# Where the norm steps between two layers stand in a slotted schedule, and one query block's delay for the second layer's input products

## The chip, the cores and the metric

The kernel runs on one core of one Trainium2 chip. The metric is the device time of a whole execution in microseconds, the median of several runs; less is better. All arithmetic is fp32.

## The reference

Eight batches of 2048 nodes with 256 features share one adjacency matrix of 2048 x 2048. Layer 0 is attention in which each of eight blocks of 256 keys has a softmax of its own, layer 1 a graph attention over all nodes. Each ends in a sum and a layer norm.

```python
q, k, v = x @ Wq.T + bq, x @ Wk.T + bk, x @ Wv.T + bv        # 4 heads of 64
scores = clip(q . k / 8, -10, 10); scores = -10 where not adjacent
ctx = sum over the 8 key blocks of softmax(scores in the block) @ v
out = layernorm(ctx @ Wo.T + bo + x) * gamma + beta
x1 = layernorm(x + out)                                       # layer 0 done
Wh = x1 @ W;  e = leaky_relu(s_src[i] + s_dst[j]), s from Wh and a
h = elu(softmax over adjacent j of e @ Wh)
result = layernorm(x1 + h)
```

## The kernel before, in words

**Slots.** Each batch b is worked in 64 slots (`SLOTS`). Slot s belongs to a query block q of 512 nodes (`NCH` = 4 blocks), a pair of heads and one of eight key blocks; a block q has 16 slots (`QS`), and i is the slot's number within its block. The order is written out by hand in the loop over s: no scheduler moves an instruction, and every engine takes its own in the order in which they are written.

**Work of every slot.** `scores(s + 1)` makes eight matmuls into `ps` (L377) and two clips with the mask into `pr` on VectorE (L388). `product(s, 0)` multiplies the probabilities of slot s with the values into `pc` (L412), which has one PSUM bank (`psC`), and ScalarE copies it to `raw` (L419). `exps(s + 1)` makes the exponentials on ScalarE (L400). Then `lower.step()` does a piece of layer 1 of the batch before: `make` builds three tiles `e` on VectorE (L712), 128 x 768 in the first third of a batch and 128 x 640 after, and `use` multiplies the three tiles built one slot earlier into `pa` (L732). `product(s, 1)` follows, with its copy. `normalize` divides by the softmax sums (`rd` on VectorE, L427, then two operations on GpSimd) in the next slot. So each engine has per slot: TensorE `ps`, `pc`, `pa`, `pc`; VectorE `rd`, two `pr`, three `e`; ScalarE `raw`, two exponentials, `raw`. Three times in 16 slots a unit of layer 1 closes: `dn` (VectorE, L755, L756), `hh` (ScalarE, L760), `ee` and `hp` (ScalarE, L764, L766) and `h` (VectorE, L768), in slots that follow each other.

**Steps between the layers.** While block q runs, `Between` finishes block q - 1, called group g = q - 1. Its steps are placed by tables from i to a step. `BESIDE` steps stand after the slot's `pr` on VectorE: `bias` (L512), `add` (attention output plus x, L538), `stats` of norm a (L477, L480; after its second half L485, L486 and a power on GpSimd, L487), `shift` (L516), `scale` (L544), `again` (L547), `stats` of norm b. `BEHIND` steps stand at the slot's end: `output` (eight matmuls into `po`, L527), `a.apply` and `finish` (four ScalarE operations each, L492; `finish` also stores the result to `x1D` in DRAM). `AHEAD` loads the stored block back in squares (`x1t`, eight loads of 64 KB), `turn` transposes the squares on VectorE (L283), and `values` multiplies a quarter of the group with layer 1's weights (`pw`, L571) and copies it to `waug` and `sd`. `po` and `pw` of the loop share one PSUM bank (`psM`). The context of layer 0 goes through DRAM in the same manner: `load_context` and `turn_context` (L454). Four groups make a batch; groups 0, 1 and 2 are finished in the blocks q = 1, 2 and 3, group 3 in a tail behind the 64 slots. SyncE issues all loads, in order.

**Groups of before.** All three have the same table: load in slot 12, turn in slot 14, `values` in slots 14 and 15 and in slots 0 and 1 of the next block. For group 2 the last two fall into the tail. Batch 0, which has no layer 1 beside it, has tables of its own (`BESIDE_0`, `BEHIND_0`, `AFTER_0`). In the last batch, layer 1 of the batch before stops 14 slots before the end of the loop (`LATE`).

Of the kernel before, what the change touches and what calls it, by code (L numbers as in the profile page):

```python
# [22 lines left out]
def adj_resnorm_kernel(  # L23
# [23 lines left out]
    NCH = N // CH  # L47
# [15 lines left out]
    QS = HP * NK  # L63
# [297 lines left out]
    def load_slab(s):  # L361
        q, hp, c = where[s]
        slab = slabs.tile([P, KT, CH], I8, tag="slab", name="slab")
        nc.sync.dma_start(out=slab, in_=clipD[q][:, KT * c : KT * (c + 1), :])
        slab_of[s] = slab

    def scores(s):
        q, hp, c = where[s]
        slab = slab_of.pop(s)
        cols = slice(q * CH, (q + 1) * CH)  # L370
        pss = []
        for u in range(KT):
            t = KT * c + u
            ps = two_banks([P, 2, CH], "ps")
            for k in range(2):
                rows = slice(k * D, (k + 1) * D)
                nc.tensor.matmul(  # L377
                    ps[:, k, :],
                    lhsT=kT[rows, hp, t * P : (t + 1) * P],
                    rhs=qT[rows, hp, cols],  # L380
                    start=True,
                    stop=True,
                )
            pss.append(ps)
        probs[s] = []
        for u in range(KT):
            pr = prp.tile([P, 2, CH], F32, tag="pr", name="pr")
            nc.vector.scalar_tensor_tensor(  # L388
                pr,
                pss[u],  # L390
                -CLIP,
                slab[:, u, :].unsqueeze(1).to_broadcast([P, 2, CH]),
                op0=ALU.max,
                op1=ALU.min,
            )
            probs[s].append(pr)
# [55 lines left out]
    def turn_context(q, hp):  # L452

        nc.vector.transpose(qT[:, hp, q * CH : (q + 1) * CH], sums.pop((q, hp))[:, 0, :])  # L454
# [46 lines left out]
    class Between:  # L501
# [87 lines left out]
    AHEAD = {12: lambda o: o.load()}  # L589
    BESIDE = {  # L590
        1: [lambda o: o.bias()],
        4: [lambda o: o.add((0, 1))],
        5: [lambda o: o.add((2, 3)), lambda o: o.a.stats((0, 1))],
        6: [lambda o: o.a.stats((2, 3)), lambda o: o.shift()],
        8: [lambda o: o.scale()],
        9: [lambda o: o.again(), lambda o: o.b2.stats((0, 1))],
        10: [lambda o: o.b2.stats((2, 3))],
        14: [lambda o: o.turn()],
    }
    BEHIND = {  # L600
        3: lambda o: o.output((0, 1)),
        4: lambda o: o.output((2, 3)),
        7: lambda o: o.a.apply(o.y),
        11: lambda o: o.finish(),
        14: lambda o: o.values((0,)),
        15: lambda o: o.values((1,)),
    }

    BESIDE_0 = {i: steps for i, steps in BESIDE.items() if i != 14} | {15: BESIDE[14]}
    BEHIND_0 = {i: step for i, step in BEHIND.items() if i != 14} | {15: BEHIND[14]}  # L610
    AFTER_0 = {i: lambda o, i=i: o.values((i + 1,)) for i in range(3)}
    AFTER = {0: lambda o: o.values((2,)), 1: lambda o: o.values((3,))}
# [271 lines left out]
    for b in range(B):  # L884
        waug = blocks.tile([P, NT, H, D1], F32, tag="waug", name="waug")
        sd = small.tile([P, 2 * H, NT], F32, tag="sd", name="sd", bufs=1)
        if b == 0:
            for s in range(3):
                load_slab(s)
            scores(0)  # L890
            for u in range(KT):
                exps(0, u)
        if lower:
            for _ in range(STEP):
                lower.make()
        closing = Closing(b - 2, CLOSING) if b > 1 else None
        if closing:
            closing.do(-1)
        group = None
        beside, behind, after = (BESIDE, BEHIND, AFTER) if b else (BESIDE_0, BEHIND_0, AFTER_0)  # L900
        for s in range(SLOTS):
            q, hp, c = where[s]
            i = s % QS
            send()
            if s + 3 < SLOTS:
                load_slab(s + 3)
            if i == 0:
                before = group
                group = Between(b, q - 1, sd, waug) if q else None
            if i == 1 and q:  # L910
                load_context(b, q - 1, 1)
            if i == QS // 2 + 1:
                load_context(b, q, 0)
            if group and i in AHEAD:
                AHEAD[i](group)
            if s == SLOTS - 3 and b + 1 < B:
                turns = [project(b + 1, g) for g in range(NCH)]
                turns[0].pop(0)()
            if s:
                normalize(s - 1)  # L920
            if s + 1 < SLOTS:
                scores(s + 1)

            if s == SLOTS - 1 and b + 1 < B:
                turns[0].pop(0)()
            if i == 3 and q:
                turn_context(q - 1, 1)
            if i == QS // 2 + 3:
                turn_context(q, 0)
            if group:  # L930
                for step in beside.get(i, ()):
                    step(group)
            elif closing:
                closing.do(s, behind=False)
            product(s, 0, not lower)
            if s + 1 < SLOTS:
                for u in range(KT):
                    exps(s + 1, u)
            if lower:
                if b + 1 < B or s < SLOTS - LATE:  # L940
                    lower.step()
            elif masks.left():
                masks.step()
            product(s, 1, not lower)

            if before and i in after:
                after[i](before)
            if i == 0 and q:
                send_context(b, q - 1, 1)
            if i == QS // 2:  # L950
                send_context(b, q, 0)
            if group and i in behind:
                behind[i](group)
            elif closing and not q:
                closing.do(s, beside=False)
        normalize(SLOTS - 1)

        send()
        before = group
        gd, fs = factors(b, sd, waug)  # L960
        group = None
        every = tuple(range(QT))

        def begin():
            nonlocal group
            group = Between(b, NCH - 1, sd, waug)

        def ctx():
            context(NCH - 1, 1)

        steps = [
            lambda: group.bias(),
            lambda: group.output(every),
            lambda: group.add(every),
            lambda: (group.shift(), group.a.stats(every)),
            lambda: group.a.apply(group.y),
            lambda: (group.scale(), group.again(), group.b2.stats(every)),
            lambda: group.finish(),
            lambda: group.turn_all(),
            lambda: group.values((0, 1)),  # L980
            lambda: group.values((2, 3)),
        ]
        if b + 1 < B:
            (k0, v0, q0), (l1, t1, k1, v1, q1), (l2, t2, k2, v2, q2), (l3, t3, k3, v3, q3) = turns
            rest = [lambda: lower.rest(1)] if lower else []
            first = [] if b else [lambda: before.values((1,))]
            order = [begin, *rest, l1, *rest, *first, lambda: before.values((2, 3))]
            order += [*rest, ctx, *rest, k0]
            order += [steps[0], t1, steps[1], v0, steps[2], steps[3], l2, k1, steps[4], q0]
            order += [steps[5], v1, t2, l3, steps[6], q1, steps[7], k2, steps[8], steps[9], t3, v2]  # L990
            order += [lambda: [load_slab(s) for s in range(3)], fs[0], q2, fs[1], k3, fs[2], v3]
            order += [lambda: scores(0), q3, lambda: [exps(0, u) for u in range(KT)]]
        else:

            step = lower.step
            order = [begin, lambda: before.values((2, 3)), steps[0], step, ctx, step, steps[1], step]
            order += [steps[2], step, steps[3], step, steps[4], step, steps[5], step, steps[6], step]
            order += [steps[7], step, steps[8], step, steps[9], step, fs[0], step, fs[1], step, fs[2]]
            order += [step, lambda: lower.rest(4)]
            assert sum(p is step for p in order) == LATE  # L1000
        for piece in order:
            send()
            piece()
        send()
        lower = Layer1(b, gd, waug)
# [56 lines left out]
```

## Time and profile before

| what | us |
|---|---|
| device time, median of 3 runs (3830.42 to 3833.37) | 3831.26 |
| profiled span | 3835.0 |
| TensorE busy with matmuls | 3696.8 |
| VectorE busy | 3203.6 |
| ScalarE busy | 1950.1 |
| GpSimd busy | 1385.1 |

A slot begins, in what follows, with the first `ps` matmul that is issued in it. The lengths below are the differences of those starts in the timeline of TensorE, in batch 3; the other batches with a layer 1 beside them agree within 0.03 us, up to a few single slots.

| slot i | 0 | 1 | 2 | 3 | 4 | 5 | 6 | 7 | 8 | 9 | 10 | 11 | 12 | 13 | 14 | 15 |
|---|---|---|---|---|---|---|---|---|---|---|---|---|---|---|---|---|
| q = 0 | 6.74 | 6.03 | 6.03 | 6.03 | 6.03 | 6.03 | 6.03 | 6.03 | 6.03 | 6.03 | 6.03 | 6.03 | 6.03 | 6.03 | 6.45 | 6.03 |
| q = 1 | 6.03 | 6.03 | 6.03 | 7.96 | 7.96 | 5.80 | 5.68 | 5.68 | 6.21 | 5.68 | 5.85 | 5.87 | 5.95 | 6.44 | 6.77 | 6.77 |
| q = 2 | 6.77 | 6.77 | 5.68 | 7.61 | 7.61 | 5.68 | 5.68 | 5.68 | 6.12 | 5.68 | 5.78 | 5.87 | 5.95 | 6.45 | 6.77 | 6.77 |
| q = 3 | 6.77 | 6.77 | 5.68 | 7.61 | 7.61 | 5.68 | 5.68 | 5.68 | 6.13 | 5.68 | 5.79 | 5.87 | 5.95 | 6.44 | | |

How to read the rows of the profile: busy time is the union of an engine's spans; a matmul's end is modelled, so TensorE shows as busy where it may be waiting on a weight load. In a timeline, a row gives the start, the time from the row's first start to its last end, engine, line, operation, names (output, then inputs) and count; brackets give the idle time before it and what ended it.

### The profile page before, as it was taken

Reading aid. Unit: us, or ns where it says so; the run is one execution under the profiler, and the core shown is the slowest. Engines: PE = TensorE matmul, PEld = TensorE weight load, DVE = VectorE, ACT = ScalarE, POOL = GpSimd, SP = SyncE. Lnnn points to the kernel's source line nnn. Section 1 sums busy time; section 2 is a strip of 40 time slices with the busy share of each in tenths; the row PEclk is TensorE's granted clock in tenths of the full one; section 3 lists DMA queues with packets and bytes.
Section 4 is the critical chain, followed back from the end, with each engine's and each line's share of the span. In section 5 each row is a group of like instructions: output and inputs, shape, how many; then the busy total and the mean of one; then the engine's idle time right before and its main releaser. Section 6 shows DMA issues by size and latency. Waiting matters only on the chain. (4 is left out here: it accounts for less than half of the span.)

```text
span 3835.0 us, 160246 instructions
## 1 busy us (share of the span) xinstructions
PE 3696.8 (96%) x72100; PEld 2752.3 (72%) x72100; DVE 3203.6 (84%) x4810; ACT 1950.1 (51%) x3601; POOL 1385.1 (36%) x1202
## 2 busy tenths in 40 slices
PE   9999999999999999999999999999999999999787
PEld 5656677776777777776777767777677777776676
DVE  5876499986999789995999959998699978998798
ACT  4666345555555555554555545555455555555321
POOL 1445233333433343343433324333343434334310
PEclk9999999999999999999999999999999999999999
DMA  6652333333333433333433334333333433333354
GB/s 161 151 113 65 77 101 99 96 87 112 105 95 102 91 117 101 97 101 87 131 99 92 98 92 134 97 95 88 110 110 94 104 86 118 104 99 86 93 149 123
DMA packets 756545, 398.50 MB, mean 104 GB/s; under 512 B 425744, under 2 KB 721040, under 8 KB 755856
## 3 DMA queue, kind: packets, MB, share of 16 engines
q1 hardware_dynamic: 705856, 354.54, 36.3%
q10 hardware_dynamic: 50000, 33.70, 2.7%
q8 instruction: 564, 9.24, 1.0%
q14 instruction: 125, 1.02, 0.1%
HBM read 331.22 MB, written 56.89 MB: 101 GB/s over the span
## 5 line engine op out<-in xcount | busy, mean ns | idle before, releaser
L388 DVE SCALAR_TENSOR_TENSOR pr<-ps,slab 128x1024 f32<-128x1024 f32 x1024 | 1192.5, 1205 | 215.7 <-PE ps L377 211.4
L712 DVE SCALAR_TENSOR_TENSOR e<-srow,gd,et 128x640 f32<-128x640 f32 (+1 forms) x1536 | 1349.1, 934 | 11.2 <-DMA srow<-rowD 5.7
L412 PEld LDWEIGHTS pc<-vaug,pr 128*64 128x64 f32 x32768 | 1040.6, 138 | 442.7 <-issue 253.7
L412 PE MATMUL pc<-vaug,pr 128*64 128x65 f32 x32768 | 1158.4, 224 | 40.9 <-ACT raw L419 32.0
L400 ACT ACTIVATE pr<-pr 128x1024 f32<-128x1024 f32 x1024 | 1050.4, 1057 | 158.1 <-DVE pr L388 143.6
L732 PE MATMUL pa<-waug,e 128*64 128x65 f32 x32768 | 1083.2, 224 | 41.1 <-DVE e L712 39.6
L732 PEld LDWEIGHTS pa<-waug,e 128*64 128x64 f32 x32768 | 1020.8, 139 | 67.7 <-DVE e L712 39.2
L377 PE MATMUL ps<-qT,kT 64*128 64x512 f32 x4096 | 1029.0, 619 | 3.6 <-DVE pr L388 2.6
L434 POOL TENSOR_TENSOR part<-raw,rd 128x512 f32<-128x512 f32 x448 | 467.9, 1044 | 1462.9 <-DVE rd L427 1450.4
L419 ACT COPY raw<-pc 128x260 f32<-128x260 f32 x1024 | 384.9, 377 | 1181.6 <-PE pc L412 1159.0
L377 PEld LDWEIGHTS ps<-qT,kT 64*128 64x128 f32 x4096 | 350.9, 186 | 330.7 <-issue 205.1
L436 POOL TENSOR_TENSOR acc<-acc,part 128x512 f32<-128x512 f32 x448 | 574.2, 1282 | 35.2
L427 DVE RECIPROCAL rd<-raw 128x8 f32<-128x8 f32 x512 | 100.9, 197 | 117.0 <-ACT raw L419 113.2
L434 POOL TENSOR_TENSOR acc<-raw,rd 128x512 f32<-128x512 f32 x64 | 66.8, 1043 | 336.9 <-DVE rd L427 336.1
L760 ACT ACTIVATE hh<-pa,dn 128x64 f32<-128x64 f32 x512 | 114.6, 320 | 100.6 <-DVE dn L756 96.8
L571 PE MATMUL pw<-w_sb,x1T 128*128 128x264 f32 x512 | 142.4, 415 | 8.6 <-DVE x1T L283 8.0
L487 POOL TENSOR_TENSOR rs_c<-rs_c,nhalf 128x4 f32<-128x4 f32 x32 | 55.6, 1737 | 228.4 <-DVE off_c L486 228.4
L321 PE MATMUL pp<-xT,wk_sb 128*128 128x512 f32 x256 | 119.0, 608 | 7.9 <-ACT qT L329 6.6
L527 PE MATMUL po<-wo_sb,qT 128*128 128x256 f32 x512 | 125.0, 389 | 1.1 <-DVE qT L454 0.8
L321 PE MATMUL pp<-xT,wq_sb 128*128 128x512 f32 x256 | 116.2, 596 | 0.0
L337 PE MATMUL pv<-wv_sb,xT 128*128 128x256 f32 x512 | 115.9, 379 | 0.0
L571 PEld LDWEIGHTS pw<-w_sb,x1T 128*128 128x128 f32 x512 | 93.5, 195 | 30.5 <-DVE x1T L283 8.7
(93 smaller groups left out, 1854.8 us busy)
## 6 DMA issues: line engine op xcount, KB each, us to landing
et<-edgeD SPq DMA_DIRECT2D x256, 320.0 KB, 3.1
slab<-clipD SPq DMA_DIRECT2D x512, 128.0 KB, 3.5
et<-edgeD SPq DMA_DIRECT2D x128, 384.0 KB, 3.5
srow<-rowD SPq DMA_DIRECT2D x64, 320.0 KB, 4.4
xg<-in_x_dram SPq DMA_DIRECT2D x32, 512.0 KB, 4.7
x1D<-y ACTq DMA_DIRECT2D x32, 512.0 KB, 3.0
x1g<-x1D SPq DMA_DIRECT2D x32, 512.0 KB, 5.6
out_dram<-o SPq DMA_DIRECT2D x32, 512.0 KB, 3.9
```

Source lines behind the costliest of these rows:

```text
L321: nc.tensor.matmul(pps[c], lhsT=w[:, kc, c * P : (c + 1) * P], rhs=st["xT"][:, kc, :], start=(kc == 0), stop=(kc == KC - 1),)
L377: nc.tensor.matmul(ps[:, k, :], lhsT=kT[rows, hp, t * P : (t + 1) * P], rhs=qT[rows, hp, cols], start=True, stop=True,)
L388: nc.vector.scalar_tensor_tensor(pr, pss[u], -CLIP, slab[:, u, :].unsqueeze(1).to_broadcast([P, 2, CH]), op0=ALU.max, op1=ALU.min,)
L400: nc.scalar.activation(pr, pr, AF.Exp, scale=0.125)
L412: nc.tensor.matmul(pc[z * D : (z + 1) * D, i, :], lhsT=probs[s][u][:, k, i * P + z * D : i * P + (z + 1) * D], rhs=vaug[:, KT * c + u, 2 * ...
L419: nc.scalar.copy(raws[s][:, k], pc)
L434: nc.gpsimd.tensor_mul(part, raw[:, :, :, :D], rd.to_broadcast([P, 2, QT, D]))
L436: nc.gpsimd.tensor_add(accv, accv, part)
L527: nc.tensor.matmul(po[:, k, :], lhsT=qT[:, c, t * P : (t + 1) * P], rhs=wo_sb[:, c, :], start=(c == 0), stop=(c == KC - 1),)
L571: nc.tensor.matmul(pw[:, k, : F + 2 * H], lhsT=self.x1T[:, c, u * P : (u + 1) * P], rhs=w1_sb[:, c, :], start=(c == 0), stop=(c == KC - 1),)
L712: nc.vector.scalar_tensor_tensor(e[:, :w], self.rows[n][:, :w], self.gd[:, h, j : j + 1], self.edge[k // JG][:, j % JG, :w], op0=ALU.max, ...
L732: nc.tensor.matmul(self.pa[z * D : (z + 1) * D, i * D1 : (i + 1) * D1], lhsT=e[:, i * P + z * D : i * P + (z + 1) * D], rhs=self.waug[:, j ...
```

## The change

For b > 0, the groups 0 and 1 (finished in q = 1 and q = 2) get a table of their own, `WIDE_BESIDE` and `WIDE_BEHIND`: the norm steps stand one to a slot where two or three stood together, `apply` comes in slot 8 and `finish` in slot 14, and the context turn of slot 11 goes to slot 14. Their stored blocks are loaded, turned and multiplied (`load`, `turn`, `values`) while the next block runs: load in slot 0, turn in slot 2, the four `values` in slots 5 to 8. Group 2 (q = 3) keeps the old table for its own steps, and in its block group 1's `load`, `turn` and `values` take place; group 3 and batch 0 are as before. No operation is added or taken away. The aim is to spread VectorE's and ScalarE's steps over the slots, and to put the extra matmuls of `values` into slots in which VectorE has much to do.

```diff
+    WIDE_BESIDE = {
+        1: [lambda o: o.bias()],
+        4: [lambda o: o.add((0, 1))],
+        5: [lambda o: o.add((2, 3))],
+        6: [lambda o: o.a.stats((0, 1))],
+        7: [lambda o: o.a.stats((2, 3))],
+        8: [lambda o: o.shift()],
+        10: [lambda o: o.scale()],
+        11: [lambda o: o.again()],
+        12: [lambda o: o.b2.stats((0, 1))],
+        13: [lambda o: o.b2.stats((2, 3))],
+    }
+    WIDE_BEHIND = {
+        3: lambda o: o.output((0, 1)),
+        4: lambda o: o.output((2, 3)),
+        8: lambda o: o.a.apply(o.y),
+        14: lambda o: o.finish(),
+    }
+    LATER_AHEAD = {0: lambda o: o.load()}
+    LATER_BESIDE = {2: lambda o: o.turn()}
+    LATER_BEHIND = {i: lambda o, i=i: o.values((i - 5,)) for i in range(5, 9)}
...
-        beside, behind, after = (BESIDE, BEHIND, AFTER) if b else (BESIDE_0, BEHIND_0, AFTER_0)
...
+                wide = b > 0 and 0 < q < NCH - 1
+                ahead = {} if wide else AHEAD
+                later_beside = {}
+                if not b:
+                    beside, behind, after = BESIDE_0, BEHIND_0, AFTER_0
+                else:
+                    beside, behind = (WIDE_BESIDE, WIDE_BEHIND) if wide else (BESIDE, BEHIND)
+                    after = {}
+                    if q > 1:
+                        later_beside, after = LATER_BESIDE, LATER_BEHIND
+            if before and later_beside and i in LATER_AHEAD:
+                LATER_AHEAD[i](before)
...
-            if i == QS // 2 + 3:
+            if i == QS // 2 + (6 if wide else 3):
                 turn_context(q, 0)
+            if before and i in later_beside:
+                later_beside[i](before)
```

More of the change, by code (lines that the diff above doesn't have):

```diff
@@ L913, in adj_resnorm_kernel @@
                 load_context(b, q, 0)
-            if group and i in AHEAD:
-                AHEAD[i](group)
+            if group and i in ahead:
+                ahead[i](group)
             if s == SLOTS - 3 and b + 1 < B:
```

## The prediction

> **What bounds the kernel now.** First the page: which engine is full, and how full the next one is.
>
> ```profile
> PE 3696.8 (96%) x72100; PEld 2752.3 (72%) x72100; DVE 3203.6 (84%) x4810; ACT 1950.1 (51%) x3601; POOL 1385.1 (36%) x1202
> PEclk9999999999999999999999999999999999999999
> ```
>
> PE is the resource to save, but DVE at 84% is close behind, so a stretch with more DVE work than average can take the lead. To see where, I cut the timeline of PE at the first score matmul (`ps`) of each slot and read the table of stretches, here for batch 3, query block q = 2, slots 6, 8, 11, 12, 13, 14 (columns: PE, PE weight loads, DVE, ACT, POOL busy, clock, DMA share, GB/s).
>
> ```profile
> 1603.14:1608.82 5.68, 5.68 (x136) 4.38 (x132) 5.65 (x13) 2.66 (x4) 2.82 (x3) 1.00 0.63 153
> ...
> 1614.51:1620.62 6.11, 5.74 (x136) 4.38 (x132) 6.11 (x7) 6.11 (x14) 2.52 (x3) 1.00 0.11 34
> ...
> 1632.09:1637.96 5.87, 5.83 (x136) 4.46 (x133) 5.83 (x13) 2.75 (x5) 4.74 (x5) 1.00 0.25 61
> 1637.96:1643.91 5.95, 5.91 (x136) 4.46 (x132) 5.92 (x10) 5.10 (x9) 2.62 (x3) 1.00 0.39 130
> 1643.91:1650.36 6.45, 5.76 (x137) 4.39 (x133) 6.45 (x9) 5.07 (x12) 2.90 (x3) 1.00 0.44 83
> 1650.36:1657.13 6.77, 6.77 (x141) 5.06 (x137) 6.77 (x10) 3.47 (x7) 2.34 (x2) 1.00 0.67 172
> ```
>
> 5.68 us is a slot in which PE never waits; slot 14 has 6.77 because it holds one `values` product, 1.09 us of PE work, and no wait. Slots 8 and 10 to 13 hold the same matmuls as slot 6 and yet take 6.11, 5.78, 5.87, 5.95 and 6.45: 1.76 us over the floor, with DVE full throughout. The timeline of PE names what ended the two large waits:
>
> ```profile
> 1616.86 1.15 PE L412 MATMUL pc<-vaug,pr 128*64 128x65 f32 x32 [0.37 <-ACT raw L419]
> ...
> 1646.59 1.15 PE L412 MATMUL pc<-vaug,pr 128*64 128x65 f32 x32 [0.69 <-ACT raw L419]
> ```
>
> The single `pc` bank was still to be copied. The timeline of ACT shows why:
>
> ```profile
> 1613.33 2.19 ACT L400 ACTIVATE pr<-pr 128x1024 f32<-128x1024 f32 x2 [0.96 <-DVE pr L388]
> 1615.42 1.12 ACT L760 ACTIVATE hh<-pa,dn 128x64 f32<-128x64 f32 x5
> 1616.41 0.40 ACT L419 COPY raw<-pc 128x260 f32<-128x260 f32 x1
> 1616.66 2.10 ACT L492 ACTIVATE y<-y,off_a,rs_a 128x256 f32<-128x256 f32 x4
> ```
>
> The copy came at 1616.41 though its matmuls had ended by 1614.6 in PE's timeline; ACT was held by `hh`, which was held by exponentials, which had waited for DVE. So the origin is DVE lateness. It is read from when DVE starts the first `pr` of a slot; these lines are slots 5, 7, 10, 11 and 14:
>
> ```profile
> 1598.63 2.35 DVE L388 SCALAR_TENSOR_TENSOR pr<-ps,slab 128x1024 f32<-128x1024 f32 x2 [2.16 <-PE ps L377]
> ...
> 1612.12 2.31 DVE L388 SCALAR_TENSOR_TENSOR pr<-ps,slab 128x1024 f32<-128x1024 f32 x2
> ...
> 1630.40 2.31 DVE L388 SCALAR_TENSOR_TENSOR pr<-ps,slab 128x1024 f32<-128x1024 f32 x2
> ...
> 1636.27 2.31 DVE L388 SCALAR_TENSOR_TENSOR pr<-ps,slab 128x1024 f32<-128x1024 f32 x2
> ...
> 1651.73 1.17 DVE L388 SCALAR_TENSOR_TENSOR pr<-ps,slab 128x1024 f32<-128x1024 f32 x1
> ```
>
> In slot 5 DVE waited 2.16 us for PE and started 1.17 after the slot did: no lateness. In slot 7 it is 1612.12 - 1608.82 - 1.17 = 2.13 late, in slots 10, 11 and 12 it is 2.92, 3.01 and 2.72, in slot 14 it is 0.20. In slots 8 and 9 it was 1.35 and 1.38 late, and slot 9 stood at the floor: some 1.4 us of lateness is free, 2 us with an `hh` and an apply close together are not, 3 us are not.
>
> **What the Trainium skill says.** "Perfetto Trace Analysis", section Optimization Strategy: look for the gaps on the most-contended engine and for the semaphore that ends them; the trace agrees, with gaps of 0.37 and 0.69 us. The same page, Optimizing Scalar/DVE Operations: an operation's profiled time is longer than the time it holds its engine, as the write acknowledgement overlaps the next one. The trace agrees: three `e` of 0.89 us each (128x640) start 2.36 us before the next instruction, so I count start to start. "PSUM — Partial Sum Buffer", section Engine vs sequencer instructions: queues of ScalarE, VectorE and GpSimdE are strict FIFO; the copy at 1616.41 behind `hh` agrees. "DMA: Bandwidth & Descriptors", section Two DMAs through the same engine are not ordered: the issuing engine must wait for the first DMA's semaphore before a dependent one; here SP's waits for `x1D<-y` before `x1t` total 194.4 us in 24 times.
>
> **The change part by part.** Nothing is added or removed: the same instructions of all engines stand in other places, for b = 1 to 7. PE's sum is unchanged, so time can only come from the waits. They are, slot by slot over 5.68: q = 1: 0.53 + 0.17 + 0.19 + 0.27 + 0.76 = 1.92; q = 2: 1.76; q = 3: 1.78, there only for b = 1 to 6, as in the last batch layer 1 has stopped by then. Together 7 x 1.92 + 7 x 1.76 + 6 x 1.78 = 36.4 us, the most that can be won here.
>
> DVE's ledger, start to start from its timeline: a plain slot is two `pr` 2.23, three `e` 2.36, `rd` 0.11, together 4.70, so 0.98 is spare. Extras: add of half a block 0.60, two statistics 0.88 (1.15 with `rs` and `off`), shift 1.14, scale 1.38, again 1.25, `x1T` turn 1.16, bias 1.13, context turn 0.63, `dn` pair 0.30, `h` 0.38. A `values` slot has 1.09 more spare, an `output` slot 1.93.
>
> Check on before, q = 2: slot 5 adds 0.60 + 0.88 - 0.98 = 0.50; slot 6 adds 1.15 + 1.14 + 0.30 - 0.98 = 1.61: 2.11 (measured 2.13). Slot 9 adds 1.25 + 0.88 + 0.38 - 0.98 = 1.53 to 1.38: 2.91 (measured 2.92). The ledger works.
>
> - *Steps spread, q = 1* (no `values` there any more, so the floor is all it has). Lateness after slot 6: 0.88 + 0.30 - 0.98 = 0.20; 7: 0.37; 8: 0.53; 9: 0; 10: 0.40; 11 (again, `dn`): 0.97; 12: 0.87; 13: 1.04; 14 (context turn moved here, `h`): 1.07; 15: 0.09. The peak of 1.07 is under the free 1.4. Gone: 1.92.
> - *q = 2*: the same, and slots 5 to 8 have 1.09 more spare each, so lateness is 0 up to slot 9, then again at most 1.07. Gone: 1.76. In slots 1 and 2 bias and turn leave 0.15 and 0.33, which `output` in slot 3 clears.
> - *q = 3*: its own steps stay, but the four `values` of the group before come in slots 5 to 8. Slot 6: 1.15 + 1.14 + 0.30 - 2.07 = 0.52; 7 and 8: 0; slot 9: 1.53; 10: 1.70; 11: 1.65; 12: 0.67. The wait in slot 8 goes; for slots 10 to 13, 1.7 stands between the free 1.4 and the costly 3, and the apply of slot 11 still precedes `hh` in slot 12. I leave 0.2 us there per block (bounds 0 and 1.34, all that those slots lose now).
> - *apply on ACT*: four of 0.49 start to start, 2.0 us, now behind slots 8 and 14 instead of 7 and 11. In slot 8 it follows `ee` and `hp` (0.72), in slot 14 nothing of layer 1, so it no longer piles on `hh` (1.0). Behind it waits the next `raw`, due 2.3 us after, needed 4.1 us after; nothing. I leave 0.1 us per block in q = 1.
> - *x1 one query block later*: eight `x1t` issues hold SP 5.12 us (SP's timeline), now from the start of slot 0, with the edge, slab and context loads queued behind; landing takes 2.3 us more (the DMA list), so slot 0 + 8 us; the turn comes in slot 2 at + 12 us. The context loads (2.83 us of issue) land near slot 1 + 8 of the 11 they have. An edge tile is ordered eight `e` (about 15 us) ahead. Nothing.
> - *`values` in slots 5 to 8*: the single `psM` bank is free, since the add of slot 5 reads `po` before; each is 1.09 us of PE wherever it stands. Nothing.
>
> Sum: 36.4 - 6 x 0.2 - 7 x 0.1 = 34.5; 3831.3 - 34.5 = 3796.8.
>
> **The rivals.** (B) Block q = 1 keeps its waits: it loses its `values`, and 1.07 us of lateness may already cost. For it: the waits in slots 12 and 13 come with falling lateness; against it: slot 9. It gives 3831.3 - 12.3 - 9.5 = 3809. (C) q = 3 gains nothing, as its steps after slot 8 are the old ones: 3831.3 - 25.8 = 3805. (D) The waits come from ACT's lumps and wander with them: 3831. Against it: slot 7's `hh` was late by DVE. (E) Slower: the DMAs bunched in slots 0 and 1 come late, and `turn` or the context turn holds DVE, with all `pr` and `e` behind it. With 3 us in each of 14 blocks and half the gain: 3831.3 + 42 - 17 = 3856. Against it: DVE waits for neither tile now, with a lead of the same two slots.
>
> **How the numbers follow.** Forecast 0.62, B 0.17, C 0.12, D 0.04, E 0.05. Faster 0.91, same 0.04, slower 0.05. The time is 3797. The range goes from 3790 (all waits gone, and a few small ones of the loads with them) to 3811, so as to take in B and C.
>
> **What would show it.** Right: slots 8 and 10 to 13 of q = 1 and 2 at 5.68 (with `values` 6.77), lateness of `pr` at most about 1.1 there and 1.7 in q = 3, PE's waits for `raw` nearly gone. Wrong: DVE waiting for `x1t` or `ctx` in slots 2 and 3, or slots 12 to 15 of q = 1 over the floor.

## The result and the profile after

| | before | after |
|---|---|---|
| device time, median (lowest to highest), 4 runs each | 3830.91 (3830.42 to 3833.37) | 3795.70 (3792.69 to 3799.87) |
| ratio, 95% interval | | 0.9908 [0.989, 0.9925] |
| TensorE busy in the profile | 3696.8 | 3678.4 |
| its waits for `raw` at `pc` (matmuls + weight loads) | 32.0 + 135.9 | 10.0 + 56.1 |

The change takes 35.2 us off, 0.9%. The page of after, part 1, has the same instruction counts on TensorE and VectorE as before, and 18.4 us less busy time on TensorE although its matmuls are the same; VectorE's fell by 8.1, the other two changed by less than 4:

```profile
PE 3678.4 (97%) x72100; PEld 2747.7 (72%) x72100; DVE 3195.5 (84%) x4810; ACT 1946.8 (51%) x3601; POOL 1387.7 (37%) x1202
```

What went is waiting, and a part of it had been shown as busy time: before, slot 11 of q = 2 has TensorE busy for 5.83 of its 5.87 us with the matmuls that take 5.68 in slot 6. The slot lengths of batch 3, found as in the table of before:

| slot i | 5 | 6 | 7 | 8 | 9 | 10 | 11 | 12 | 13 | 14 | 15 |
|---|---|---|---|---|---|---|---|---|---|---|---|
| q = 1 | 5.80 | 5.68 | 5.68 | 5.68 | 5.68 | 5.68 | 5.68 | 5.68 | 5.68 | 5.68 | 5.68 |
| q = 2 | 6.77 | 6.77 | 6.77 | 6.77 | 5.68 | 5.68 | 5.68 | 5.68 | 5.68 | 5.68 | 5.68 |
| q = 3 | 6.77 | 6.77 | 6.77 | 6.77 | 5.68 | 5.68 | 5.68 | 5.68 | 5.70 | | |

Every slot is at 5.68 (5.70 once), or at 6.77 where a `values` product stands; slot 5 of q = 1 has 5.80 in both kernels, as it holds 64 matmuls of `pa` and not 60. The table of stretches for slots 7, 8, 12 and 13 of q = 1 (columns as in the prediction) shows TensorE without a gap, while VectorE is as full as it was:

```profile
1489.94:1495.62 5.68, 5.68 (x137) 4.38 (x133) 5.64 (x13) 2.89 (x6) 3.15 (x3) 1.00 0.31 84
1495.62:1501.30 5.68, 5.68 (x136) 4.38 (x132) 5.68 (x7) 3.77 (x10) 3.85 (x4) 1.00 0.01 3
1518.35:1524.04 5.69, 5.69 (x137) 4.39 (x133) 5.66 (x12) 2.52 (x4) 2.33 (x2) 1.00 0.07 22
1524.04:1529.72 5.68, 5.68 (x137) 4.38 (x133) 5.68 (x11) 3.88 (x10) 2.33 (x2) 1.00 0.33 84
```

Full is not the same as late. In the timeline of VectorE, the first `pr` of those slots:

```profile
1491.32 2.31 DVE L388 SCALAR_TENSOR_TENSOR pr<-ps,slab 128x1024 f32<-128x1024 f32 x2
1497.19 2.31 DVE L388 SCALAR_TENSOR_TENSOR pr<-ps,slab 128x1024 f32<-128x1024 f32 x2
...
1520.99 2.31 DVE L388 SCALAR_TENSOR_TENSOR pr<-ps,slab 128x1024 f32<-128x1024 f32 x2
1526.57 2.32 DVE L388 SCALAR_TENSOR_TENSOR pr<-ps,slab 128x1024 f32<-128x1024 f32 x2
```

Less the slot's start and 1.17, they are 0.21, 0.40, 1.47 and 1.36 us late; before it was 2.01, 1.44, 2.72 and 1.71 in q = 1. In q = 3, whose own steps did not move, lateness in slots 10 to 12 is 1.61, 1.80 and 1.70, where it was 2.93, 3.01 and 2.73. The timeline of ScalarE around the `hh` of that block, the place of the largest wait of before:

```profile
1720.70 2.19 ACT L400 ACTIVATE pr<-pr 128x1024 f32<-128x1024 f32 x2 [0.28 <-DVE pr L388]
1722.80 1.12 ACT L782 ACTIVATE hh<-pa,dn 128x64 f32<-128x64 f32 x5
1723.78 0.40 ACT L419 COPY raw<-pc 128x260 f32<-128x260 f32 x1
```

The copy comes 1.48 us into slot 13 (1722.30), and TensorE asks for the bank 1.92 us into it, so the copy is done just in time. In the same block of before the copy came 2.23 us into slot 13 (1744.81), after TensorE had asked:

```profile
1747.04 0.40 ACT L419 COPY raw<-pc 128x260 f32<-128x260 f32 x1
```

Summed over batches 1 to 7 in the two profiles, from the first `ps` of a block to that of the next (q = 3 to its slot 14), q = 1 went from 705.5 to 676.5, q = 2 from 706.3 to 693.9 and q = 3 from 598.4 to 602.7, as the `values` products moved on by a block; 37.1 us less in all, 0.7 of it in two single slots of before that were longer than in its other batches. The two profiled spans differ by 44.1 us, but 7 of these are in batch 0, which the change doesn't touch and which varies by some us from run to run.

### The profile page after: what moved, and what is told of

The parts are those of the page before. It is cut to its first block, busy times and chain, and to the rows that moved or that the text cites. A ratio compares the mean times of both kernels' runs of the same rounds, so it can differ in the third digit from the quotient of the medians.

```text
span 3790.9 us, 160217 instructions
## 1 busy us (share of the span) xinstructions
PE 3678.4 (97%) x72100; PEld 2747.7 (72%) x72100; DVE 3195.5 (84%) x4810; ACT 1946.8 (51%) x3601; POOL 1387.7 (37%) x1202
## 3 DMA queue, kind: packets, MB, share of 16 engines
q14 instruction: 125, 1.02, 0.1%
## 5 line engine op out<-in xcount | busy, mean ns | idle before, releaser
L436 POOL TENSOR_TENSOR acc<-acc,part 128x512 f32<-128x512 f32 x448 | 574.9, 1283 | 35.2
L487 POOL TENSOR_TENSOR rs_c<-rs_c,nhalf 128x4 f32<-128x4 f32 x32 | 55.6, 1737 | 229.6 <-DVE off_c L486 229.6
```

Of the source, the lines that this page charges most:

```text
L436: nc.gpsimd.tensor_add(accv, accv, part)
```

## The experiments

**Theory 1** (the prediction's): VectorE falls late where steps stand together and nothing gives it time; its lateness passes through the exponentials to the copy of `pc`; each block follows its own ledger. **Rival A**: moving `values` does everything. **Rival B**: spreading does everything. **Rival D**: the waits are ScalarE's own lumps, `apply` near `hh`. (A and B are letters of the experiments; the prediction's B was that q = 1 keeps its waits. D is the same in both.) In the diffs below the unchanged context is that of the changed kernel unless another is named.

**e1: later, not spread.**

```diff
-    WIDE_BESIDE = {...}
-    WIDE_BEHIND = {...}
+    WIDE_BESIDE = {i: steps for i, steps in BESIDE.items() if i != 14}
+    WIDE_BEHIND = {i: step for i, step in BEHIND.items() if i < 14}
...
-            if i == QS // 2 + (6 if wide else 3):
+            if i == QS // 2 + 3:
```

> Half of the change: x1 of groups 0 and 1 is loaded, turned and multiplied in the next block (load in slot 0, turn in 2, values in 5 to 8), but the norm steps stay in their old slots (finish in 11, context turn in 11). Theory 1 (VectorE's lateness makes the waits, each block by its own ledger): q = 1 has the old steps and no values, so its waits stay at 0.53 + 0.17 + 0.19 + 0.27 + 0.76 = 1.92 us a block, with pr 2.0 and 3.0 us late in slots 7 and 11; q = 2 has old steps over values slots, as q = 3 of the changed kernel has, and is at the floor. Loss against the changed kernel 7 x 1.92 = 13.4: about 3809. Rival A (where values stands does everything, spreading is idle): 3796. Rival B (spreading does everything): q = 1 and q = 2 keep their waits, 3796 + 26 = 3822.

Measured: 3807.81 us, ratio to before 0.9936 [0.9922, 0.9951]. In q = 1 slots 8 and 10 to 13 take 6.21, 5.86, 5.87, 5.96, 6.44, the lengths of before; q = 2 and q = 3 are at the floor. So moving `values` isn't enough in q = 1, and spreading isn't needed in q = 2: A and B both fall, and each block followed its own ledger. Spreading alone, with `values` in its old places, was not run. Slot 8 of q = 1 in this run's table of stretches:

```profile
1500.36:1506.57 6.21, 5.75 (x136) 4.38 (x132) 6.06 (x7) 6.21 (x15) 2.41 (x3) 1.00 0.10 32
```

**e2: all of the change, help in other slots.**

```diff
-    LATER_BEHIND = {i: lambda o, i=i: o.values((i - 5,)) for i in range(5, 9)}
+    LATER_BEHIND = {i: lambda o, i=i: o.values((i - 10,)) for i in range(10, 14)}
```

> The whole change, but values of groups 0 and 1 in slots 10 to 13 of the next block instead of 5 to 8. Theory 1: q = 1 and q = 2 stay at the floor, since spread steps need no help (q = 2 then has the lateness of q = 1, at most about 1.6 us). q = 3, with its old steps, is late again by 2.1 us in slot 7, so its slot 8 takes 6.1 us (0.44 over), and slots 10 to 13 are at their new floor of 6.77 or within 0.1 of it. Loss 6 x 0.5 = 3 us: about 3799. Rival A (the slots 5 to 8 for values are what counts): q = 2 and q = 3 lose most of what they won, about 3796 + 20 = 3816.

Measured: 3799.99 us, ratio 0.9915 [0.9899, 0.9932]. q = 1 and q = 2 are at the floor; q = 3 has `pr` 2.13 us late in slot 7, 6.12 in slot 8 and 6.87 in slot 10 (0.10 over 6.77), the rest of the slots from 5 on at the floor; its slot 0 takes 5.68 to 6.80, differently in each batch. For spread steps the place of `values` is idle; for clustered ones it must come beside the cluster.

**e3: the first norm's cluster put back in groups 0 and 1.**

```diff
-        5: [lambda o: o.add((2, 3))],
-        6: [lambda o: o.a.stats((0, 1))],
-        7: [lambda o: o.a.stats((2, 3))],
-        8: [lambda o: o.shift()],
+        5: [lambda o: o.add((2, 3)), lambda o: o.a.stats((0, 1))],
+        6: [lambda o: o.a.stats((2, 3)), lambda o: o.shift()],
...
-        8: lambda o: o.a.apply(o.y),
+        7: lambda o: o.a.apply(o.y),
```

> The whole change, but the first norm of groups 0 and 1 has its old places back: statistics in slots 5 and 6, shift in 6, apply behind slot 7; the second norm stays spread. Theory 1: in q = 1, pr is 2.0 us late in slot 7 and slot 8 takes about 6.2 (0.53 over); slots 10 to 13 stay at 5.68, as VectorE has caught up by then. In q = 2 the values in slots 5 to 8 take it up: no wait. Loss 7 x 0.53 = 3.7 us. Rival D (the waits come from ScalarE's lumps, apply close to hh, and not from VectorE): slot 8 over the floor in both q = 1 and q = 2.

Measured: one run, 3797.21 us. Slot 8 of q = 1 takes 6.20 (lateness in slot 7: 2.01), slots 6, 7 and 9 to 15 take 5.68; q = 2 has no wait, though `apply` stands behind slot 7 there too. D expected it there.

**e4: the same, `apply` away from `hh`.** As e3, with `apply` back at 8.

> As the run with the first norm's old places, but apply stays behind slot 8, away from hh. Theory 1: the copy of pc that the product of slot 8 waits for stands behind the late exponentials and hh, before any apply, so the wait in slot 8 of q = 1 stays, at about 0.4 us. Rival D (apply is what stands in the way): slot 8 is back at 5.68.

Measured: one run, 3799.91 us. Slot 8 of q = 1 takes 6.21, from 1498.96 to 1505.17. First the timeline of ScalarE, then TensorE's:

```profile
1497.67 2.19 ACT L400 ACTIVATE pr<-pr 128x1024 f32<-128x1024 f32 x2 [0.85 <-DVE pr L388]
1499.76 1.32 ACT L780 ACTIVATE hh<-pa,dn 128x64 f32<-128x64 f32 x6
1500.94 0.41 ACT L419 COPY raw<-pc 128x260 f32<-128x260 f32 x1
```

```profile
1501.40 1.15 PE L412 MATMUL pc<-vaug,pr 128*64 128x65 f32 x32 [0.46 <-ACT raw L419]
```

The wait is there without any `apply` in between: late `pr`, exponentials, `hh`, copy, `pc`. D falls as far as `apply` goes; `hh` is work of ScalarE too, and the next runs show its part.

**e5: the kernel before with 1.14 us less on VectorE.** The sum with beta is missing from groups 0 to 2 here.

```diff
-        6: [lambda o: o.a.stats((2, 3)), lambda o: o.shift()],
+        6: [lambda o: o.a.stats((2, 3))],
```

> The kernel before, with the shift step (1.14 us of VectorE) left out of the groups finished inside the loop, so that beta and the output bias are missing from their sum; nothing else moves, and ScalarE and TensorE do what they did. Theory 1 by the ledger for q = 2: late 0.5 in slot 6, 1.0 in slot 7, 0 and 0.4 in 8 and 9, then 1.9, 2.1 and 2.0 in slots 10 to 12. Slot 8 at 5.68; slots 10 to 13 over by 0.0 to 0.3 in all. So about 1.5 of the 1.8 us a block go: 20 blocks x 1.5 = 30, about 3801. Rival D (ScalarE's lumps): the waits of slots 8 and 13 stay, gain under 8 us.

Measured: 3807.70 us, ratio 0.9939 [0.9923, 0.9956]. Slot 8 went to 5.68 and slots 10 to 12 to 5.68 (5.70 once), with lateness in q = 2 of 1.00 in slot 7, as forecast, and of 2.23, 2.41 and 2.31 in slots 10 to 12, where 1.9, 2.1 and 2.0 were forecast. But slot 13 stayed at 6.44, 6.30 and 6.31 in q = 1, 2 and 3: I had allowed it 0.3 at most, so the gain is 24 us and not the 30 of the forecast. TensorE's timeline in slot 13 of q = 2 (from 1627.99):

```profile
1630.52 1.15 PE L412 MATMUL pc<-vaug,pr 128*64 128x65 f32 x32 [0.55 <-ACT raw L419]
```

So lateness of 2.4 is free in slots 10 and 11 and 2.3 costs 0.62 in slot 12. What slot 12 has, and slot 7, is `hh`.

**e6 and e7: one and two VectorE operations more in slot 6.**

```diff
-        6: [lambda o: o.a.stats((0, 1))],
+        6: [lambda o: o.a.stats((0, 1)), lambda o: o.same()],
...
+        def same(self):
+            nc.vector.tensor_tensor(self.r, self.r, self.r, ALU.max)
```

e7 calls `same` twice.

> The changed kernel with one more VectorE operation of 128 x 1024 (a maximum of a tile with itself, about 1.13 us) in slot 6 of q = 1 and q = 2. Theory 1: in q = 1 the lateness from slot 7 on rises by 1.1, to about 1.3 in slot 7, 1.5 in slot 8, 1.9 in slot 9, 2.6 in slots 12 to 15; small waits in slots 12 to 14, under 0.5 us a block in all. In q = 2 the values slots swallow it: no wait. Rival (VectorE's lateness is of no account at this size): no wait in q = 1 either; rival D: the same.

> The same with two such operations, 2.26 us. Theory 1: q = 1 is late by 2.5 in slot 7 and would reach 3.8 by slot 12, so it runs into waits of 1 to 2 us a block, in slot 8 and in slots 10 to 14, until the lateness stands near 3. q = 2 has 4 x (0.98 + 1.09) of room in slots 5 to 8 against 0.60 + 0.88 + 0.30 + 1.15 + 1.14 + 2.26 of work: no wait. Rival D: no wait at all.

Measured, one run each: 3802.48 and 3809.76 us. q = 2 is at the floor in both, as forecast. In q = 1, e6 waits in one slot alone: slot 13 takes 6.61 (0.93 over, more than the 0.5 I gave it), after a lateness of 2.62 in slot 12. e7 waits in two: slot 8 takes 6.80 after 2.61 in slot 7, slot 13 takes 6.75 after 2.76 in slot 12; slots 10 to 12, for which I had forecast waits, stand at 5.68. In these two runs the wait comes only behind an `hh`, and it is then lateness less a constant:

| where | `hh` of | late in its slot | next slot over the floor | difference |
|---|---|---|---|---|
| before, q = 1, slot 7 | 6 | 2.01 | 0.53 | 1.48 |
| e7, q = 1, slot 7 | 6 | 2.61 | 1.12 | 1.49 |
| before, q = 2, slot 7 | 5 | 2.13 | 0.44 | 1.69 |
| before, q = 1, slot 12 | 5 | 2.72 | 0.76 | 1.96 |
| e5, q = 2, slot 12 | 5 | 2.31 | 0.62 | 1.69 |
| e6, q = 1, slot 12 | 5 | 2.62 | 0.93 | 1.69 |
| e7, q = 1, slot 12 | 5 | 2.76 | 1.07 | 1.69 |
| after, q = 3, slot 12 | 5 | 1.70 | 0.02 | 1.68 |

The constant can be counted from the start of a slot, in before's timelines for slot 7 of q = 2: 1.17 to the first `pr`, 1.21 from there to the first exponential, 2.09 for the two, 0.99 for five `hh`, 0.45 from the copy's start to the product: 5.91 plus lateness. The product is due at 5.68 + 1.92 = 7.60. That leaves 1.69, and a sixth `hh` (0.20) takes its own time off. Before, slot 12 was itself 0.27 over the floor, so the product of slot 13 was due 0.27 later: 1.96 - 0.27 = 1.69.

Slots 10 to 12 of before lost 0.10, 0.19 and 0.27 in q = 2 without an `hh` in front of them. There the traces show a second and shorter way, which neither the prediction nor Theory 1 has: TensorE needs the third `e` of the slot before, and VectorE, being late, has just made it. VectorE's and TensorE's timelines of before, for slot 10 of q = 2 (from 1626.31):

```profile
1627.90 2.47 DVE L712 SCALAR_TENSOR_TENSOR e<-srow,gd,et 128x640 f32<-128x640 f32 x3
```

```profile
1629.21 2.02 PE L732 MATMUL pa<-waug,e 128*64 128x65 f32 x60
```

The third `e` ended at 1630.37, the first matmul that reads it began at 1630.42, and `pa` took 2.02 where it took 1.92 in slot 6: that is the whole 0.10 of slot 10. In slot 11 this way costs 0.08 and the first `pc` 0.11. In slot 12 the first `pc` costs 0.11, and the second 0.16, as the copy that it waits for stood behind the four operations of `finish` and the issue of its store on ScalarE. So of the 1.76 us of q = 2 some 0.18 came through `e` and 0.16 in this last way; the origin, late VectorE, is the same.

**e8: half a dose, to test the rule ahead.**

```diff
+            nc.vector.tensor_tensor(self.r[:, :2], self.r[:, :2], self.r[:, :2], ALU.max)
```

`same` stands in slot 6 as in e6.

> The changed kernel with one more VectorE operation of half the size (128 x 512, about 0.6 us) in slot 6 of q = 1 and q = 2. The runs so far suggest a rule: if hh is written in a slot, the next slot waits for what the lateness of pr in that slot exceeds 1.69 us (hh of five) or 1.49 us (hh of six). Theory 1 with this rule: in q = 1 lateness in slot 7 is 0.21 + 0.6 = 0.8, no wait in slot 8; in slot 12 it is 1.47 + 0.6 = 2.05, so slot 13 takes 5.68 + 0.36 = 6.04; no other slot waits. q = 2: none. A plain limit on lateness of 2.4 to 3 us, whatever ScalarE does: no wait anywhere.

Measured: one run, 3800.47 us. Lateness is 0.81 in slot 7 and 2.07 in slot 12; slot 13 takes 6.07, and no other slot of q = 1 or q = 2 is over. The two timelines, VectorE's `pr` in slot 12 (from 1522.71) and TensorE's `pc` in slot 13 (from 1528.39):

```profile
1525.95 2.31 DVE L388 SCALAR_TENSOR_TENSOR pr<-ps,slab 128x1024 f32<-128x1024 f32 x2
```

```profile
1530.70 1.15 PE L412 MATMUL pc<-vaug,pr 128*64 128x65 f32 x32 [0.31 <-ACT raw L419]
```

1525.95 - 1522.71 - 1.17 = 2.07, less 1.69 is 0.38; measured 0.39 over the floor. A limit on lateness alone is ruled out: 2.07 costs time here, and 2.41 cost none in slot 11 of e5.

**e9: the same cause in another place.** Slot 14 of q = 0 is over the floor by 0.41 in both kernels; the last closing group's steps stand in slots 11 to 13. There is no `hh` in slot 13, but `ee` and `hp` stand between the exponentials and the copy (0.82 us in ScalarE's timeline of after). Counted as above, with a slot of 6.03, they leave 2.20 free; 2.65 was late, so some 0.45 was to be expected.

```diff
-        11: [(3, "add")],
-        12: [(3, "stats")],
-        13: [(3, "finish")],
+        12: [(3, "add")],
+        13: [(3, "stats")],
+        15: [(3, "finish")],
```

> The changed kernel with the last closing group of q = 0 (sum in slot 11, statistics in 12, finish in 13) moved to slots 12, 13 and 15. Theory 1: the 0.41 us over the floor in slot 14 of q = 0 (batches 2 to 6; 0.5 in each of slots 13 and 14 of batch 7) have the same cause, pr 2.65 us late in slot 13; lateness there falls below 1.5 and slot 14 goes to 6.03. Gain about 3 us in all. If the wait is ScalarE's (finish and ee, hp together), it moves with finish to slot 15 or to slot 0 of the next block.

Measured: one run, 3797.48 us. In batches 2 to 6 slot 14 and slot 15 are at 6.03, and slot 0 of the next block too: the wait went, it didn't move. But slot 1 of q = 1 took 7.07 in batch 5, where the changed kernel has 6.03; the cause of this stays open, and it came again in e12. Over batches 1 to 7, q = 0 has 1.4 us less and q = 1 has 1.1 more than in the first profile of the changed kernel. In batch 3 lateness in slot 13 fell from 2.65 to 1.08. In batch 7, where all of q = 0 is later, slot 13 went from 6.51 to 6.03 and slot 14 from 6.58 to 6.22, while 0.14 and 0.06 appeared in slots 5 and 8. The one time can't tell so small a gain: this run's batch 0 was 4.9 us longer than in the first profile of the changed kernel.

**e10, e11, e12: a version meant to beat both.** In the last batch layer 1 ends 14 slots early. The two products of a slot then follow each other, and the second waits for the one bank to be copied. The later closing steps of e9 are in e10 and e12 too.

```diff
+            alone = 2 if b + 1 == B and s >= SLOTS - LATE else not lower
-            product(s, 0, not lower)
+            product(s, 0, alone)
...
-            product(s, 1, not lower)
+            product(s, 1, alone)
...
-        pool, tag = (psL, "psL") if alone and k else (psC, "psC")
+        pool, tag = {0: (psC, "psC"), 1: (psL, "psL"), 2: (psM, "psM")}[int(alone) if k else 0]
```

> A version that should beat both kernels: the later closing steps, and in the last batch's 14 slots without layer 1 (q = 3, slots 2 to 15) a second bank for the product's second half (psM), since with no layer 1 between the two products the second waits for the copy of the first: 4.68 us a slot where batch 0 with two banks takes 3.93. Theory: slots 2 and 9 to 13 gain 0.7 each, slots 3 to 8 less, as output and values share psM; together 5 to 8 us, with the closing steps 8 to 11: about 3786.

> The changed kernel itself, unaltered, beside the version above on one chip: the same waits as in its first profile, about 3796.

Measured: e10 3796.99 us (0.9908 [0.9893, 0.9922]), e11 3794.61 us (0.9902 [0.9885, 0.9918]) on the same chip: no gain. Slots 2 and 3 of e10's last block in the table of stretches, and what TensorE waited for in slot 3:

```profile
3450.79:3454.72 3.93, 3.93 (x76) 2.63 (x72) 3.93 (x6) 1.81 (x7) 2.22 (x2) 1.00 0.94 185
3454.72:3462.46 7.74, 5.93 (x84) 4.08 (x81) 4.21 (x6) 4.37 (x7) 3.87 (x5) 1.00 0.25 82
```

```profile
3460.54 1.78 PE L527 MATMUL po<-wo_sb,qT 128*128 128x256 f32 x7 [1.81 <-ACT raw L419]
```

Slots 2 and 9 to 12 gained 0.75 or more as meant, but `po` now waits 1.81 us for the product's copy to free the bank they share: slot 3 takes 7.74 where the changed kernel has 6.61. I had taken such a slot for a smaller gain; it is a loss. So the bank is borrowed only where nothing else wants it:

```diff
-            alone = 2 if b + 1 == B and s >= SLOTS - LATE else not lower
+            alone = 2 if b + 1 == B and q == NCH - 1 and i in (2, 9, 10, 11, 12, 13) else not lower
```

> As the version with the later closing steps and the second bank in the last batch, but with that bank only in slots 2 and 9 to 13 of its q = 3, in which neither output nor values wants it. Theory: those slots take 3.93 to 4.6 instead of 4.68 to 5.01, and slots 3 to 8 go back to 6.61 and 5.77 from the 6.85 to 8.50 of the run before, in which the shared bank made TensorE wait for copies and sums of its own. Against the changed kernel 4 us there and 1 to 3 us in q = 0: about 3789, 0.15% under it, near the edge of what the times can tell; the slot lengths will tell.

Measured: 3788.66 us (3787.06 to 3789.71), ratio to before 0.9887 [0.987, 0.9903]. Slots 2 and 3 of its last block:

```profile
3451.74:3455.67 3.93, 3.93 (x76) 2.63 (x72) 3.93 (x6) 1.82 (x7) 2.23 (x2) 1.00 0.92 184
3455.67:3462.28 6.61, 6.08 (x84) 4.15 (x80) 4.21 (x6) 4.36 (x7) 2.86 (x4) 1.00 0.33 107
```

In this profile q = 3 sums to 598.7 over batches 1 to 7 (602.7 in the changed kernel) and q = 0 to 681.7 (683.7), while q = 1 has 1.1 more: 4.9 us less. Its runs lie under all eight of the changed kernel (3792.69 to 3799.87), though the two were not run side by side, and the intervals of their ratios to the kernel before overlap.

## Why the prediction was right, point by point

- **The sum.** Forecast 3797 (34.5 us off), measured 3795.7 (35.2 us off). That the effect is in waits of q = 1 to 3 holds: in the profiles they fell by 37.1 us, against 36.4 counted beforehand in one batch and multiplied out.
- **q = 1, steps spread.** The waits went, with lateness at most 1.58 where I had 1.07. The peak of "at most about 1.1" did not hold. The mis-sized terms are above all shift and again: I had 1.14 and 1.25 start to start and they took 1.35 and 1.42 here, for a reason proposed in the last section; `h` in slot 9 took 0.46 where I had 0.38, as it closes a unit of six. It is in part luck that this did no harm: 1.58 is over the 1.4 that I took for free, but it came in slots without an `hh`, where more is free; in slot 12, which has one, lateness was 1.47 of the 1.69 that are free. The 0.1 us a block that I left for `apply` wasn't needed.
- **q = 2.** As worked out: at the floor, lateness 1.05 at most (forecast 1.07).
- **q = 3.** Lateness in slots 9 to 12 was 0, 1.61, 1.80, 1.70 and 0.96 in slot 13, against 0, 1.53, 1.70, 1.65 and 0.67. I left 0.2 us of wait and there was 0.01 to 0.02. It is close to the edge all the same: by the table above, 1.69 was free there.
- **The allowance of some 1.4 us of lateness.** The weak step, right for the verdict and wrong as a rule. It came from slots 8 and 9, which have no `hh`; the runs put a limit of 1.49 or 1.69 in its place for slots with an `hh`, while 2.4 was free in slots without one. Nor is the copy of `pc` the only way: 0.18 of the 1.76 us in q = 2 came through `e`, a way that the prediction doesn't have. Both ways begin with VectorE's lateness, so the sum of the waits held.
- **Transfers and banks at nothing.** VectorE waited for neither `x1t` nor `ctx` in the trace of after (its idle time before both turns is nil), and `values` in slots 5 to 8 made 6.77 each, which is 5.68 + 1.09. Rival E didn't come.
- **Rivals B and C.** q = 1 does keep its waits if the steps aren't spread (e1), and q = 3 does lose in slot 8 if help comes late (e2); in the change as made neither happened. D is ruled out for `apply` by e3 and e4, and waits that go with VectorE's work alone (e5 to e8) speak against it; what is true in it is that ScalarE's own work, `hh` above all, sets how much lateness is free.

## What to carry to other kernels

An engine that isn't the fullest on the average can still set the pace where its work stands in clusters. Count its backlog slot by slot, from start-to-start times, and compare it with what the chain behind it can absorb: that limit is a sum of a few durations and differs from slot to slot. Work of the bound engine itself, such as `values`, which cost the same 1.09 us in its old and in its new places, is best put beside the clusters; and before a bank is borrowed, look at who fills it next.

## What the runs showed of the hardware

VectorE operations with both inputs in SBUF and operations of GpSimd lengthened each other here. "SBUF — State Buffer", section Who interferes with whom, says that a VectorE instruction with two SBUF inputs contends with a GpSimd instruction that reads SBUF; the traces agree, and show that the cost depends on the pair. The trace of after, GpSimd and then VectorE, in slot 11 of q = 2:

```profile
1614.55 1.28 POOL L436 TENSOR_TENSOR acc<-acc,part 128x512 f32<-128x512 f32 x1
```

```profile
1615.42 1.48 DVE L547 TENSOR_TENSOR y<-y,xg 128x1024 f32<-128x1024 f32 x1
```

`again` began 0.41 us before GpSimd's sum ended and took 1.48; with no GpSimd operation beside it, it took 1.21 to 1.23. The same holds for `e`, which has two inputs in SBUF as well: 0.88 us as a rule, 1.08 (the median of 75 in the trace of before, tiles of 128 x 640) where it began while that sum ran. The power (L487) didn't slow `e`: beside it `e` kept its 0.88, in 45 cases of before. Nor did the sum slow `pr`, which has its other input in PSUM: beside it 1.22 (the median of 117), and 1.22 without. The other way round, the power of the first norm took 1.02 with VectorE idle, 1.99 beside `shift` in before and 1.66 beside three `e` in after:

```profile
866.15 1.02 POOL L487 TENSOR_TENSOR rs_a<-rs_a,nhalf 128x4 f32<-128x4 f32 x1 [12.00 <-DVE off_a L486]
```

```profile
1608.32 1.99 POOL L487 TENSOR_TENSOR rs_a<-rs_a,nhalf 128x4 f32<-128x4 f32 x1 [0.84 <-DVE off_a L486]
```

```profile
1494.79 1.66 POOL L487 TENSOR_TENSOR rs_a<-rs_a,nhalf 128x4 f32<-128x4 f32 x1 [0.84 <-DVE off_a L486]
```

So VectorE lost 0.2 to 0.3 us beside the sum and nothing beside the power, while the power lost 0.6 to 1.0 and the sum next to nothing (1.29 beside `e`, 1.27 without). This fits the ledger's misses in q = 1: `shift` and `again` took 0.21 and 0.17 more than it has, and there they met the sum. `scale` had met it in before already, which is in the ledger's 1.38; in q = 2 of after it took 1.13 start to start. That the meeting is the cause was read from the traces and not tried by itself.
